# A shared expert cut into five parts per batch and handed out from a queue

## The chip, the cores and the metric

The kernel runs on one core of a Trainium2 chip. The metric is the device time of one execution in microseconds (us). The kernel before takes 3459.9 us, the median of three runs (3458.05 to 3460.16).

## The reference

Two decoder layers over a batch of 8 sequences of 256 tokens, width 512, all in 32-bit floats. Every layer adds attention, cross-attention and a feed-forward block to the running `x`, each behind a layernorm. The change lies in the feed-forward block of layer 0, a mixture of 64 experts with six chosen per token and a capacity of 192 tokens per expert, plus a shared expert that every token passes through:

```python
logits = x @ gate_weight.T          # softmax, best 3 of 8 groups, best 6 experts
slot = flat * C + jnp.minimum(pos, C - 1)
buf = jnp.zeros((E * C, H)).at[slot].set(x[tok]).reshape(E, C, H)
out = einsum(silu(buf @ Wg) * (buf @ Wu), Wd)
y = jnp.sum(out[slot] * topk_w, axis=1)
shared = jax.nn.silu(x @ Sg.T) * (x @ Su.T) @ Sd.T      # 512 -> 704 -> 512
return y + shared
```

Here `x` is the layernormed input of the block. `Sg` and `Su` are 704 x 512, `Sd` is 512 x 704.

## The kernel before

The kernel runs six stages one after the other: self-attention, cross-attention of layer 0 (`l0_cross`, which also carries the front half of the mixture), the experts (`l0_experts`), the state-space attention of layer 1 (`l1_mamba`), cross-attention of layer 1, and the last feed-forward block. `x` stays on the chip as 16 tiles of 128 tokens, two per batch.

Work is recorded in program order. A framework then orders the instructions of each engine; instructions given to `self.pin` (all matrix products, the products `hT`, the additions of the shared result to `x`, the shared weights' loads) keep the order in which the program records them. Each engine, and the DMA queue of SyncE (SP), runs its instructions in order.

`l0_cross` works in rounds, one per batch `b`, of eight slots `s`; there are 8 + 3 rounds, since later steps of a batch lag behind (L628 and on). A slot computes one part of the attention scores (`scores`: products, an exp on ScalarE, three VectorE passes), the outputs of the slot two before, and then what the list `between[s]` holds. An entry there is a pair: how far ahead or behind the round's batch it works, and the step. So `(1, turn)` transposes the next batch, `(-1, result)` projects the attention output of the batch before and adds it to `x` by way of ScalarE, VectorE and GpSimd, and `(-2, ...)` are the steps of the mixture's front (`l0_front`, L676) for the batch whose attention is done: `normal` (layernorm, and a copy to device memory), `turn` (transpose to `xnT`), `route` (gate products, top-k), `slots` (a place in the expert's buffer for every choice). `scatter` writes the tokens' numbers to two maps in device memory with indirect DMAs on GpSimd, two per call and twelve per batch; `last` adds one more behind the last batch and loads the maps, from which `slots` in the narrower sense, the list of tokens per expert, is summed.

The shared expert of a batch has six steps `hidden(b, m)` (L830), one per block of 118 of the 704 hidden features (the last has 114), and two steps `down(b, i)` (L846), one per 128 tokens. A hidden step is eight products into one bank, a silu on ScalarE and a product on VectorE; a down step is six products and an addition to `x`. The list `between` places them by hand: `hidden` 0 to 3 in slots 6 and 7 of round b + 2, 4 and 5 in slot 0 of round b + 3, the two downs in slots 2 and 3. Its weights are loaded once, ahead of the rounds, into four tiles of the weight pool (L683 to L696): Sg and Su in halves of 704 KB, and Sd in six slabs of 118 rows (the last 114) of 512 features; the first four slabs share the four tiles.

`l0_experts` takes the experts in pairs: it gathers the tokens (GpSimd, indirect), transposes them, loads each expert's weights through the same pool of eight tiles, and writes the results to `y_d` in device memory (L962, L977). `l1_mamba` then runs `combine` (L663) batch by batch: twelve indirect gathers of `y_d` per batch into a ring of six tiles `ye`, each added to `x` on VectorE. The layernorm of the first batch, with a power on GpSimd's queue (L153), and the transposes (L1040) follow.

Of the kernel before, what the change touches and what calls it, by code (L numbers as in the profile page):

```python
# [18 lines left out]
P = 128  # L19
# [49 lines left out]
class Decoder:  # L69
# [352 lines left out]
    def l0_cross(self, front):  # L422
# [11 lines left out]
        with ExitStack() as ctx:  # L434
# [169 lines left out]
            for i in range(2):  # L604
# [4 lines left out]
            hidden = lambda m: [(-2 - m // 4, lambda b, m=m + i: moe["hidden"](b, m)) for i in range(2)]  # L609
            between = (  # L610
                [(1, lambda b: features(b, "k", 0)), *hidden(4)],
                [(1, lambda b: features(b, "k", 1)), (1, lambda b: values(b, 0))],
                [(-3, lambda b: moe["down"](b, 0)), (1, lambda b: values(b, 1)), (-2, moe["normal"])],
                [(-3, lambda b: moe["down"](b, 1)), (1, turn)],
                [(-1, lambda b: divide(b, 0)), (1, lambda b: features(b, "q", 0)), (-2, moe["turn"])],
                [(-1, lambda b: divide(b, 1)), (-2, moe["route"]), (1, lambda b: features(b, "q", 1)), (2, context)],
                [(-1, lambda b: result(b, 0)), *hidden(0), (-2, moe["slots"])],
                [(-1, lambda b: result(b, 1)), *hidden(2)],
            )

            for n in range(6):
                s, i, k = (7 + n) % 8, n // 3, n % 3 * 2
                between[s].append((
                    -2 if s == 7 else -3,
                    lambda b, i=i, k=k: moe["scatter"](b, i, k) if b < B - 1 else None,
                ))

            for b in range(B + 3):  # L628
                for s in range(8):
# [7 lines left out]
                    for d, work in between[s]:  # L637
                        if 0 <= b + d < B:
                            work(b + d)
                            if work is moe["slots"] and b + d == B - 1:  # L640
                                for n in range(6):
                                    moe["scatter"](B - 1, n // 3, n % 3 * 2)
                                moe["last"]()

# [3 lines left out]
    def l0_moe(self, outer):  # L648
# [9 lines left out]
        self.l0_cross(lambda *pools: self.l0_front(*pools, xn_d, topw, read, slots))  # L658
        with ExitStack() as ctx:
            self.ps = ctx.enter_context(self.psum("ps"))  # L660
            self.l0_experts(ctx.enter_context(self.pool("c2")), xn_d, slots, y_d)
# [14 lines left out]
    def l0_front(self, one, pool, bank, xn_d, topw, read, slots):  # L676
# [3 lines left out]


        n_m = -(-MS // MB)
        rows = lambda m: min(MB, MS - m * MB)  # L683
        up, sd = {"g": [], "u": []}, []
        for n, name in (("g", "Sg"), ("u", "Su")):
            for c in range(2):
                t = self.wpool.tile([P, 2048], F32, tag="w", name="w")
                v = t[:, : 2 * MS].rearrange("p (c m) -> p c m", c=2)
                self.pin(nc.sync.dma_start(v, a[name][2 * c * P : 2 * (c + 1) * P, :].rearrange("(c p) m -> p c m", p=P)))
                up[n].append(v)  # L690
                m = len(sd)
                sd.append(t[:MB, 2 * MS : 2 * MS + D])
                self.pin(nc.sync.dma_start(sd[m], a["Sd"][m * MB : (m + 1) * MB, :]))
        for m in range(4, n_m):
            sd.append(one.tile([P, D], F32, name=f"sd{m}")[: rows(m), :])
            self.pin(nc.sync.dma_start(sd[m], a["Sd"][m * MB : m * MB + rows(m), :]))  # L696
# [3 lines left out]
        zero = one.tile([P, NSC], I32, name="zero")  # L700
# [20 lines left out]
        def turn(b):  # L721
            xnT = work[b]["xnT"] = pool.tile([P, HC, S], F32, tag="mT", name="mT", bufs=1)
            for i, xn in enumerate(work[b]["xn"]):
# [4 lines left out]
                nc.scalar.copy(xnT[:, :, i * P : (i + 1) * P], t.rearrange("p (c t) -> p c t", c=HC))  # L728

# [11 lines left out]
        def slot(b):  # L741
# [3 lines left out]
            pos = pool.tile([P, 2, E0], F32, tag="pos_e", name="pos_e", bufs=1)  # L745
# [12 lines left out]
            past = pool.tile([P, 2, E0], F32, tag="past", name="past", bufs=1)  # L758
# [70 lines left out]

        def hidden(b, m):  # L830
            w = work[b]
            if m == 0:
                w["hT"] = pool.tile([P, n_m, S], F32, tag="hT", name="hT", bufs=1)
            n = rows(m)
            t = bank()
            for h, name in enumerate("gu"):
                for c in range(HC):
                    self.mm(
                        t[:n, h * S : (h + 1) * S], up[name][c // 2][:, c % 2, m * MB : m * MB + n],
                        w["xnT"][:, c, :], c == 0, c == HC - 1,  # L840
                    )
            act = pool.tile([P, S], F32, tag="act", name="act")
            nc.scalar.activation(act[:n], t[:n, :S], AF.Silu)
            self.pin(nc.vector.tensor_tensor(w["hT"][:n, m, :], act[:n], t[:n, S:], ALU.mult))  # L844
# [795 lines left out]
```

## Time and profile before

| What | us |
|---|---|
| median of three runs | 3459.9 |
| the profiled execution | 3465.64 |
| its span | 3463.9 |
| cross-attention of layer 0 with the mixture's front, 415.6 to 1149.3 | 733.7 |
| TensorE busy in it | 669.2 |
| experts, 1149.3 to 1951.7 | 802.4 |
| TensorE busy in it | 802.4 |
| behind the experts to mamba's first transposes, 1951.7 to 1980.3 | 28.6 |

The profile is of one execution. TensorE is busy for 3247 of 3463.9 us, VectorE for 1598.5, ScalarE for 998.6, GpSimd for 758.5. A row of the profile names an engine (PE is TensorE, DVE VectorE, ACT ScalarE, POOL GpSimd, SPq the DMA queue of SyncE), the line of the kernel, the operation and the tiles it writes and reads. All matrix products stand under L100, the helper that records them, and count twice in "x"; tell them apart by their tiles: `mm<-mT,w` are the shared expert's hidden products, `mm<-w,hT` and `mm<-sd,hT` its downs, `sc<-xgT,w` the experts'. What stands in square brackets is the engine's idle time just before the row, and what ended it.

### The profile page before, as it was taken

To read this page: it belongs to the slowest core of one execution; us is meant where nothing else is said; L and a number is where in the kernel's file an instruction comes from. 1 tells how busy PE (TensorE), PEld (TensorE's weight loads), DVE (VectorE), ACT (ScalarE), POOL (GpSimd) and SP (SyncE) were. 2 spreads that over 40 slices of the span, in tenths; PEclk is the share of its full clock that TensorE was granted. 3 is DMA by queue.
4 is the path that set the end of the run, shared out by engine and by line. 5 is a ranking of instruction groups with operands and counts; after the bars stand their busy time and mean duration, and the time that the engine had idled before them with its cause. 6 is when DMAs were issued, how large, how long until landed. Compare 5 with 4: busy or idle time off the path is not lost.

```text
span 3463.9 us, 47107 instructions
## 1 busy us (share of the span) xinstructions
PE 3247.0 (94%) x18803; PEld 2114.8 (61%) x18803; DVE 1598.5 (46%) x3784; ACT 998.6 (29%) x1959; POOL 758.5 (22%) x792
## 2 busy tenths in 40 slices
PE   7999878999999899999999578998999899999999
PEld 5666545666666687878787455563444566666665
DVE  4555589888875000000000288655666333333332
ACT  1222223333342122222222133442555322222221
POOL 3222001222235211111110276322121111111111
PEclk9999989999999999999999778997999899999999
DMA  4000010000100677777777743011000000000000
GB/s 175 1 1 1 7 64 16 13 13 13 35 7 21 198 234 236 237 236 242 232 245 224 223 140 91 1 33 50 26 26 17 34 7 6 7 7 1 7 6 13
DMA packets 106812, 272.57 MB, mean 79 GB/s; under 512 B 15136, under 2 KB 23968, under 8 KB 105696
## 3 DMA queue, kind: packets, MB, share of 16 engines
q1 hardware_dynamic: 88128, 219.16, 19.3%
q0 software_dynamic: 18464, 50.40, 5.2%
q8 instruction: 148, 2.42, 0.3%
q14 instruction: 72, 0.59, 0.1%
HBM read 235.81 MB, written 33.70 MB: 78 GB/s over the span
## 4 chain that ended last, share of the span: by engine, by line
PE 67%; DVE 12%; POOL 3%; issue 2%; DMA 2%; ACT 1%; SPq 0%; POOLq 0%; DVEq 0%; ACTq 0%
PE mm L100 18%; PE sc L100 15%; PE out L100 7%; PE w L100 6%; PE s L100 4%; PE a L100 3%; PE b L100 3%; PE sums L100 2%; PE acc L100 2%; PE st L100 2%; DVE e L526 1%; PE pt L926 1%; PE rt L100 1%; POOL ye L667 1%; DVE acc L1066 1%
## 5 line engine op out<-in xcount | busy, mean ns | idle before, releaser
L100 PE MATMUL sc<-xgT,w 128*112 128x192 f32 (+1 forms) x3072 | 529.6, 328 | 0.0
L100 PEld LDWEIGHTS sc<-xgT,w 128*112 128x112 f32 (+1 forms) x3072 | 497.4, 182 | 41.1 <-issue 40.9
L952 DVE TENSOR_TENSOR aT<-act,sc 112x192 f32<-112x192 f32 (+1 forms) x192 | 68.0, 354 | 741.3 <-ACT act L951 741.3
L100 PE MATMUL mm<-xnT,w 128*128 128x256 f32 x1152 | 280.9, 401 | 7.4 <-ACT xnT L252 5.9
L100 PE MATMUL mm<-w,aT 112*128 112x512 f32 (+3 forms) x768 | 262.7, 596 | 0.0
L100 PEld LDWEIGHTS mm<-xnT,w 128*128 128x128 f32 x1152 | 227.2, 201 | 46.2 <-ACT xnT L252 8.2
L100 PE MATMUL w<-xnT,w 128*128 128x256 f32 x1024 | 242.9, 380 | 0.0
L100 PE MATMUL out<-w,mix 128*128 128x512 f32 x512 | 240.4, 592 | 0.0
L1483 DVE TENSOR_TENSOR h<-base,b 128x512 f32<-128x512 f32 x128 | 88.0, 687 | 327.4 <-PE b L100 327.4
L916 POOL DMA_INDIRECT xg<-xn_d,slots x96 | 90.9, 947 | 641.2 <-PE pt L926 634.8
L100 PEld LDWEIGHTS w<-xnT,w 128*128 128x128 f32 x1024 | 192.2, 190 | 61.1 <-issue 40.7
L1487 POOL TENSOR_TENSOR mix<-h 128x256 f32<-128x256 f32 x128 | 93.1, 727 | 610.4 <-DVE h L1485 549.6
L1344 DVE TENSOR_REDUCE m<-s 128x1 f32<-128x512 f32 x256 | 164.6, 685 | 102.3 <-PE s L100 83.5
L153 POOL TENSOR_TENSOR lnr<-lne,c_nhalf 128x1 f32<-128x1 f32 x112 | 66.6, 596 | 645.7 <-DVE lne L151 639.5
L100 PE MATMUL st<-q,k 32*128 32x256 f32 (+1 forms) x1024 | 196.6, 545 | 1.2 <-ACT e L522 1.2
L100 PE MATMUL mm<-mT,w 128*118 128x256 f32 (+1 forms) x768 | 175.2, 388 | 9.8 <-DVE hT L844 9.8
L1293 ACT ACTIVATE e<-st 128x512 f32<-128x512 f32 x256 | 138.9, 595 | 141.9 <-PE st L100 140.2
L951 ACT ACTIVATE act<-sc 112x192 f32<-112x192 f32 (+1 forms) x192 | 63.6, 331 | 402.0 <-PE sc L100 402.0
L100 PEld LDWEIGHTS out<-w,mix 128*128 128x128 f32 x512 | 97.3, 190 | 122.4 <-issue 120.5
L100 PEld LDWEIGHTS mm<-w,aT 112*128 112x128 f32 (+3 forms) x768 | 95.6, 163 | 122.5 <-issue 122.5
L100 PEld LDWEIGHTS mm<-mT,w 128*118 128x118 f32 (+1 forms) x768 | 141.9, 186 | 45.9 <-DVE hT L844 12.1
L100 PE MATMUL s<-k,q 32*128 32x512 f32 x512 | 159.9, 700 | 6.3 <-issue 3.5
(333 smaller groups left out, 5315.1 us busy)
## 6 DMA issues: line engine op xcount, KB each, us to landing
w<-in_Wg SPq DMA_DIRECT2D x64, 704.0 KB, 7.7
w<-in_Wu SPq DMA_DIRECT2D x64, 704.0 KB, 4.6
w<-in_Wd SPq DMA_DIRECT2D x64, 448.0 KB, 6.4
w<-in_Wd SPq DMA_DIRECT2D x64, 256.0 KB, 5.4
y_d<-yo SPq DMA_DIRECT2D x64, 256.0 KB, 3.9
y_d<-yo SPq DMA_DIRECT2D x64, 128.0 KB, 4.1
w<-in_W SPq DMA_DIRECT2D x8, 1024.0 KB, 5.5
x<-in_x SPq DMA_DIRECT2D x16, 256.0 KB, 5.8
```

What stands on the lines that cost most here:

```text
L100: self.pin(self.nc.tensor.matmul(out, lhs, rhs, start=start, stop=stop))
L153: ins = nc.gpsimd.tensor_tensor(r, e, self.nhalf[:, :n], ALU.pow)
L526: self.pin(nc.vector.scalar_tensor_tensor(e, e, 1.0, low, ALU.max, ALU.mult))
L667: nc.gpsimd.indirect_dma_start(y, None, y_d, bass.IndirectOffsetOnAxis(ap=read[:, k, i : i + 1], axis=0))
L916: nc.gpsimd.indirect_dma_start(xg, None, xn_d, bass.IndirectOffsetOnAxis(ap=slots[:, i : i + 1], axis=0))
L926: self.pin(nc.tensor.transpose(t[:, blk], w[n][:, blk], self.ident))
L951: nc.scalar.activation(act[:n_m], ps[:n_m, :CAP], AF.Silu)
L952: nc.vector.tensor_tensor(w["a", h][:n_m, m, :], act[:n_m], ps[:n_m, S : S + CAP], ALU.mult)
L1293: nc.scalar.activation(w["e"][kc][:, j, :], st, AF.Exp, scale=SCALE)
L1344: nc.vector.tensor_reduce(m, sc, AX.X, ALU.max)
L1483: nc.vector.tensor_tensor(both(h), twice(base), both(t), ALU.add)
L1487: nc.gpsimd.tensor_tensor(mix, h[:, :G], h[:, G:], ALU.add)
```

## The change

The eight steps become five parts: three of two hidden steps each and two downs (`shared_parts`). The parts of batches 0 to 6 wait in one queue, in order. The list `between` has four places `(0, None)`, in slots 0, 2, 6 and 7; from slot 7 of round 2 on each takes the next part from the queue. When the last batch's `slots` and `scatter` are recorded (round 9, slot 6), what is left in the queue is recorded behind them. The last batch's parts are not in the queue: its `xnT` is written to device memory, read back in the experts' stage, the shared weights are loaded once more behind the last expert's, and its five parts stand behind the last expert.

To make room, several small tiles share the buffer of others: `zero`, `pos_e`, `past`, the silu's output (from two buffers to one, `gated`), and the transposes of the last two batches (in the ring of the softmax tiles). The transposes of the other batches get two buffers.

The diff, cut to its core (deleted functions moved unchanged are left out):

```diff
-            hidden = lambda m: [(-2 - m // 4, lambda b, m=m + i: moe["hidden"](b, m)) for i in range(2)]
             between = (
-                [(1, lambda b: features(b, "k", 0)), *hidden(4)],
+                [(1, lambda b: features(b, "k", 0)), (0, None)],
                 [(1, lambda b: features(b, "k", 1)), (1, lambda b: values(b, 0))],
-                [(-3, lambda b: moe["down"](b, 0)), (1, lambda b: values(b, 1)), (-2, moe["normal"])],
-                [(-3, lambda b: moe["down"](b, 1)), (1, turn)],
+                [(0, None), (1, lambda b: values(b, 1)), (-2, moe["normal"])],
+                [(1, turn)],
...
-                [(-1, lambda b: result(b, 0)), *hidden(0), (-2, moe["slots"])],
-                [(-1, lambda b: result(b, 1)), *hidden(2)],
+                [(-1, lambda b: result(b, 0)), (0, None), (-2, moe["slots"])],
+                [(-1, lambda b: result(b, 1)), (0, None)],
             )
...
+            parts = iter([
+                lambda b=b, work=work: work(b) for b in range(B - 1) for work in self.shared_parts(*moe["shared"])
+            ])
...
                     for d, work in between[s]:
-                        if 0 <= b + d < B:
+                        if work is None:
+                            if 8 * b + s >= 23:
+                                next(parts, lambda: None)()
+                        elif 0 <= b + d < B:
                             work(b + d)
                             if work is moe["slots"] and b + d == B - 1:
                                 for n in range(6):
                                     moe["scatter"](B - 1, n // 3, n % 3 * 2)
                                 moe["last"]()
+                                for part in parts:
+                                    part()
...
         def turn(b):
-            xnT = work[b]["xnT"] = pool.tile([P, HC, S], F32, tag="mT", name="mT", bufs=1)
+            xnT = work[b]["xnT"] = pool.tile([P, HC, S], F32, tag="mT" if b < B - 2 else "e", name="mT", bufs=2 if b < B - 2 else 3)
...
+            if b == B - 1:
+                nc.sync.dma_start(end, xnT)
...
-            act = pool.tile([P, S], F32, tag="act", name="act")
+            act = pool.tile([P, S], F32, tag="gated", name="gated", bufs=1)
             nc.scalar.activation(act[:n], t[:n, :S], AF.Silu)
-            self.pin(nc.vector.tensor_tensor(w["hT"][:n, m, :], act[:n], t[:n, S:], ALU.mult))
+            self.pin(nc.vector.tensor_tensor(made["hT"][:n, m, :], act[:n], t[:n, S:], ALU.mult))
+
+        def two(b, m):
+            hidden(b, m)
+            hidden(b, m + 1)
...
+        return (
+            *(lambda b, m=m: two(b, m) for m in range(0, n_m, 2)), *(lambda b, i=i: down(b, i) for i in range(2)),
+        )
...
                 late = [lambda pair=pair, h=h: first(pair, h)]
                 if h == 1:
                     late.append(lambda pair=pair: last(pair))
+        weights = self.shared_weights(pool)
+        xnT = pool.tile([P, HC, S], F32, tag="xnT", name="xnT", bufs=1)
+        nc.sync.dma_start(xnT, end)
         for work in late:
             work()
+        for part in self.shared_parts(pool, lambda: self.bank("sc"), weights, lambda b: xnT):
+            part(B - 1)
```

`shared_weights` issues the ten loads that `l0_front` issued before, in the same order: half of Sg, a slab of Sd, the other half, a slab, the same with Su, then the last two slabs, all pinned.

## The prediction

> **What bounds the kernel now.** I read the page, then the engines' busy time in stretches, then each engine's instructions in order around the two places where the change puts work.
>
> ```profile
> PE 3247.0 (94%) x18803; PEld 2114.8 (61%) x18803; DVE 1598.5 (46%) x3784; ACT 998.6 (29%) x1959; POOL 758.5 (22%) x792
> ...
> PE 67%; DVE 12%; POOL 3%; issue 2%; DMA 2%; ACT 1%; SPq 0%; POOLq 0%; DVEq 0%; ACTq 0%
> ```
>
> TensorE carries two thirds of the chain that ended last, so work removed from it can pay, but only where VectorE isn't as full. The cross-attention round of batch 4 (719.95 to 805.5, 85.5 us), cut at its eight slots; the columns are stretch, length, then busy time (count) of PE, weight load, DVE, ACT and POOL, granted clock, DMA share, GB/s:
>
> ```profile
> 740.88:751.31 10.43, 10.43 (x46) 4.44 (x45) 9.27 (x18) 1.03 (x1) 3.41 (x4) 1.00 0.01 1
> 751.31:759.18 7.87, 7.87 (x46) 3.86 (x45) 5.53 (x13) 1.98 (x4) 1.12 (x2) 1.00 0.10 35
> 774.80:788.90 14.10, 13.42 (x77) 9.09 (x78) 13.11 (x37) 3.80 (x6) 0.00 (x0) 1.00 0.06 20
> 788.90:805.50 16.60, 14.12 (x68) 9.03 (x67) 14.24 (x31) 9.31 (x16) 4.48 (x4) 0.90 0.00 0
> ```
>
> These are slots 2, 3, 6 and 7. Over the round PE is busy 82.1, DVE 71.0; slots 3 to 7 take 54.2 and hold 47.0 of DVE. TensorE bounds the round, with DVE close behind in its second half. The two gaps in TensorE's order of work around the experts:
>
> ```profile
> 1112.86 13.98 PE L100 MATMUL mm<-mT,w 128*118 128x256 f32 x64
> 1149.29 2.88 PE L926 MATMUL pt<-c_const,xg 128*128 128x128 f32 x12 [12.14 <-DMA xg<-xn_d,slots]
> ...
> 1946.25 5.47 PE L100 MATMUL mm<-w,aT 128*128 128x512 f32 x18
> 1980.32 1.11 PE L1040 MATMUL pt<-c_const,xn 128*128 128x128 f32 x4 [28.60 <-DVE xn L169]
> ```
>
> 12.1 us are idle before the experts and 28.6 behind them. In the second, the combine runs on POOL and DVE (its first add, its seventh gather):
>
> ```profile
> 1964.63 0.75 DVE L670 SCALAR_TENSOR_TENSOR x<-ye,topw,x 128x512 f32<-128x512 f32 x1 [17.46 <-DMA ye<-y_d,read]
> ...
> 1969.45 1.17 POOL L667 DMA_INDIRECT ye<-y_d,read  x1 [0.30 <-issue]
> ```
>
> And the shared weights, loaded once in the cross stage (SP's order; the stretch while only the tail of these loads is under way; landing):
>
> ```profile
> 445.30 0.41 SPq L689 DMA_DIRECT2D w<-in_Sg  x1
> 454.40 5.52 SPq L689 DMA_DIRECT2D w<-in_Su  x1
> ...
> 468.00:472.00 4.00, 4.00 (x39) 2.06 (x41) 3.90 (x7) 2.17 (x5) 0.00 (x0) 1.00 0.13 50
> w<-in_Sg SPq DMA_DIRECT2D x2, 704.0 KB, 11.0
> w<-in_Su SPq DMA_DIRECT2D x2, 704.0 KB, 16.6
> ```
>
> DMA share 0.13 at 50 GB/s is two of 16 engines. The last Su lands 454.4 + 16.6 = 471.0, 25.7 us behind the first issue; the stream is dry at about 482. SP held the first Su back to 452.7 for its buffer, but these two engines never ran empty (51 GB/s at 456 to 460, with nothing else in flight), so the hold doesn't set the landing.
>
> **The price of one batch's shared expert.** Batch 7's lies bare at 1103.94 to 1137.1: six hidden blocks 7.0 + 13.9 = 20.9, two down products 10.5 (1126.68 on), 31.4 us of PE. A pair of blocks is 7.0, a down 5.2.
>
> **Front: up to the last attention result.** Ahead of result(7,1) (ends 1076.3) TensorE now does six batches and a pair, 6 x 31.4 + 7.0 = 195.4. After, 24 parts stand there: four batches, three pairs and a down, 125.6 + 26.2 = 151.8. So 43.6 us leave TensorE. Not all is gained. Per round 5.2 leave slot 3, and a pair in 6 or 7 becomes a down (1.8) or slot 2's down a pair (-1.8). Slots 3 to 7 then hold 42 to 46 us of PE beside 46.3 of DVE (hT and x adds move with the parts, 0.41 and 0.69 each). Round 2 (546 to 634), which has little shared work, shows that regime: its slots 3 to 7 took 63.1 for 56.7 of DVE, 90%. 46.3/0.9 = 51.4, so a round gains 2.8 there, at best 5.2. By round: 2 (round 2, slot 6 is DVE's: 16.46 of 17.80), 3, 3, 4.5, then 6.4 in round 6 (no context to clean, DVE 66 of 80), 4.3 in round 7 (slot 3 falls back on the exp-DVE chain, as slots 1 and 2 now do), 4.7 in round 8: 27.9. The gate tile has one buffer, not two: the second silu waits for the first product and the next exp stands behind it on ACT, 1 to 1.5 us where DVE lags; I take 3 for all. 25 gained; bounds 15 (DVE at 90% everywhere) and 43.6 (TensorE bounds all).
>
> **Front: from there to the experts.** result(7,1) to the slots products is 34.6 us now (1076.3 to 1110.9) and stays: it is the layernorm chain of x (POOL's pow at +21.6 behind the scatters), then top-k; TensorE has 19.4 us to do under it (a down, two pairs), so it idles some 4 us, +1 for a half clock. Behind the slots stand seven parts in the built program, five of batch 6 and two downs of batch 5: 1.9 + 31.4 + 10.5 = 43.8. Now the experts start 38.3 behind the slots (1111.0 to 1149.3), waiting for 13 scatters, the map and the gather. So +5.5; but without the idle gap the first expert isn't at half clock: x48 took 9.62 against 8.05, x12 2.88 against 1.8, -2.6. Net +3.9. **Experts start 25 - 3.9 = 21 us earlier.** Nothing of the shared expert is issued on POOL; ACT, with 239 of 734 us busy in this stage, takes its silus between exps as before. Hidden: the write of xnT (512 KB, on SP ahead of the map's loads, done before the scatters), its read (512 KB at 236 GB/s, 2 us, where the DMA share is 0.74), the tags reused by zero, pos_e and past (freed a round before); uncovered they would cost 2 us each.
>
> **Back.** Times as if the experts had not moved. The ten shared loads (4.3 MB) are pinned behind the y_d write of 1941.86, so they issue from 1942.2, and the last two y_d writes, Wz, Wxbc and wout stand behind them on SP's queue. When does the second Su land? Row one, the expert weights on this queue: 4.6 to 7.7 us from issue to landing, 360 to 386 GB/s in the stretch 1936 to 1944; so the 3.6 MB up to that Su by 1955, and TensorE runs straight on and ends at 1983.8. Row two, the same loads at 445: +25.7, so 1967.9. The Trainium skill decides ("DMA: Bandwidth & Descriptors", in "Why a DMA increments its semaphore by 16 and not by 1"): a copy uses the largest number of engines up to 16 that divides its slowest dimension. Sd comes in slabs of 118 rows, 2 x 59, so two engines: 242 KB at 49 GB/s is 4.9 us each, and Sg and Su have a sixteenth on these engines, behind them. That is a property of the load, not of the cross stage. I take row two. It also lets the y_d writes land only near 1979 (36.7 behind, as the stream at 482), not at 1961.
>
> Beside that batch 7 brings six silus on ACT (2.1 of 28.6 us busy there) and 3.8 us on DVE. Wz to wout now issue one by one as the Sd slabs land, the last near 1976, and take some 5.6 us each; mamba first needs them behind 2012: hidden, and worth that wait if mamba were to start before 1985.
>
> TensorE: gate of block 0, then idle to 1967.9; 0.9 + 17.5 for the rest of the blocks, 10.5 down. Clock: rows show half clock lasting on after a gap, 8.85 for 7.07 (711.2), 5.89 for 3.70 (986.9), 616.5 to 622.7: 1.8 to 3.1 lost. The skill ("TensorE: Matmul & The Clock Gate", Part 1) gives one window of 3.4 us, 1.7 lost. I take the rows, 2.4. End 1999.2. On DVE's queue both x adds stand ahead of all the combine's adds (built order): the first is at 2000.2, not 1964.63. Six gathers fit the buffers; the seventh waits for the first add: 2000.95 against 1969.45, +31.5. The pow behind the thirteenth gather, xn and mamba's first transposes follow at the same pace: **mamba starts at 2011.8, +31.5.** W1 (4 MB) now loads at 1996 to 2010 beside the gathers; gathers beside weights took 6.5 us against 3.7: +2 (0 to 4). Behind that everything keeps its order. **Back +33.5** (28 to 40).
>
> **Sum.** -21 + 33.5 = +12.5 on the profiled 3465.6 (span 3463.9 and 1.7 around it): 3478.1. The median of the runs is 5.7 lower: 3459.9 + 12.5 = **3472.4**.
>
> **Rivals.** (A) The shared weights land as expert weights do, by 1955: first add at 1984.7, seventh gather 1985.5, +16 and 2.5 of contention; -21 + 18.5 = -2.5, 3457.4. Against it: the rows at 445. (B) Not slower: TensorE bounds the whole front, as PE 82.1 of 85.5 in round 4 suggests; 43.6 - 3.9 = 39.7, less 33.5: -6.2, 3453.7. It decides once the front gains over 37.4. Against: DVE at 13.1 of 14.1 and 14.2 of 16.6. With (A) too it would be -21. (C) DVE sets the front's pace fully and the half-clock gaps multiply: gain 15 - 3.9 = 11; +22.5, 3482. (D) The parts don't fill the gaps at all: the seven only lengthen the wait, batch 7's only follows its weights; that is the forecast's own reading behind the experts, and with a front of 15 it is (C).
>
> **How the numbers follow.** Forecast 0.57, C 0.18, A 0.13, B 0.12 (half of it with A's arrival in part). 0.2% is 7 us, about what a measurement can tell. Faster: a third of A and half of B, 0.10; same: the rest of A and B and the forecast's low edge, 0.19; slower 0.71. Range from A, 3457, to past C with a back of 37: 3486. The likeliest's own: 3464 to 3481.
>
> **What would show it.** Right: experts start near 1128, PE has no gap ahead of them; behind them PE waits some 14 us for DMA w<-in_Su within the first hidden block; x_83's add stands ahead of the first combine add, 35 us later after the experts' end than now; PE idle ahead of mamba falls to about 12. Wrong: Su landing within 14 us of the first issue; rounds 3 to 5 shorter by over 6 or under 2 us; any wait of the experts on weights (e1's now load without the 12 us lead).

## The result

| | before | after |
|---|---|---|
| median of 6 runs, us | 3461.28 (3458.05 to 3465.86) | 3487.75 (3483.22 to 3490.96) |
| profiled execution, its span | 3465.64, 3463.9 | 3487.53, 3485.8 |

After / before is 1.0076 (95% interval 1.0065 to 1.0087): **26.5 us slower**. The forecast was +12.5. Executions of one kernel differ by some 4 us to either side, so a difference of a few us between two medians of four runs shows nothing here.

The profiled execution of before reached the cross stage 4.6 us later than that of after (first score product at 441.68 and 437.08), in a stage that the change doesn't touch. Stages are therefore compared by their lengths. Five points of the trace cut the time: the first score product of the cross stage, the end of result(7,1), the end of the first 48 expert products, the end of the last expert product, mamba's first transposes.

| stretch | before | after | difference | forecast |
|---|---|---|---|---|
| cross stage up to result(7,1) | 634.8 | 622.0 | -12.8 | -25 |
| result(7,1) to the end of the first expert products | 85.1 | 92.2 | +7.1 | +3.9 |
| experts | 790.1 | 790.1 | 0 | 0 |
| last expert product to mamba's transposes | 28.6 | 60.4 | +31.8 | +31.5 |
| from there to the end | 1483.5 | 1483.9 | +0.4 | +2 |
| sum | | | +26.5 | +12.5 |

The sum equals the difference of the medians. So the back, the last two stretches, came near its forecast (+32.2 for +33.5), and the front, the first two, gained 6 us where 21 were expected.

The page of after, engines and chain:

```profile
PE 3254.9 (93%) x18803; PEld 2117.2 (61%) x18803; DVE 1595.2 (46%) x3784; ACT 990.0 (28%) x1953; POOL 764.4 (22%) x792
...
PE 64%; DVE 14%; issue 3%; POOL 2%; DMA 2%; ACT 2%; SPq 0%; POOLq 0%; DVEq 0%; ACTq 0%
```

TensorE has the same 18803 products as before, but is busy 7.9 us longer, and its share of the chain fell from 67% to 64%: waits on DVE and half clock took the place of products.

**The front.** Round 4 of after, slots 2 to 7, each cut 0.7 us behind the slot's first score product (columns: stretch, length, then busy time and count of PE, weight load, DVE, ACT and POOL, granted clock, DMA share, GB/s):

```profile
724.57:737.17 12.60, 12.44 (x70) 7.90 (x72) 11.97 (x24) 2.69 (x3) 2.45 (x3) 1.00 0.01 2
737.17:742.14 4.97, 3.02 (x38) 1.56 (x40) 4.32 (x9) 3.44 (x6) 0.97 (x1) 1.00 0.01 0
742.14:754.81 12.67, 7.72 (x55) 5.81 (x52) 10.84 (x22) 3.59 (x7) 6.33 (x6) 0.82 0.12 44
754.81:764.13 9.32, 9.32 (x72) 6.47 (x68) 6.47 (x24) 2.69 (x8) 2.21 (x2) 0.88 0.09 28
764.13:777.95 13.82, 13.51 (x81) 9.12 (x82) 12.92 (x34) 3.10 (x5) 0.00 (x0) 1.00 0.06 20
777.95:791.96 14.01, 10.96 (x51) 4.28 (x52) 13.34 (x28) 7.50 (x12) 5.11 (x4) 1.00 0.00 0
```

Slots 4 and 5 of the same round before:

```profile
759.18:766.74 7.56, 7.25 (x53) 5.36 (x52) 7.16 (x13) 3.01 (x6) 4.38 (x4) 1.00 0.10 35
766.74:774.80 8.06, 8.06 (x65) 6.35 (x65) 6.98 (x22) 2.73 (x8) 2.33 (x2) 1.00 0.11 33
```

Slot 2 grew from 10.43 to 12.60 (a pair where a down stood), slot 3 fell from 7.87 to 4.97, and slot 4 grew from 7.56 to 12.67, of which TensorE works 7.72. The clock drops there and stays down in slot 5. The round took 89.1 us against 85.5, with one part less. What TensorE waited for in rounds 3 to 5 of after (engine and instruction, releaser, us in total, times, longest), and below the dots the counterpart of the first line before:

```profile
PE mm L722 <- DVE o L569: 14.4, 3, 5.0
PE mm L100 <- DVE hT L875: 5.5, 3, 2.5
PE st L100 <- ACT e L522: 2.4, 2, 1.2
PE mm L100 <- ACT raw L496: 2.4, 1, 2.4
...
PE mm L727 <- DVE o L569: 0.9, 3, 0.3
```

The first line is where most of the added waiting lies: the second transposes of the layernormed x in slot 4 wait for DVE's o product, 4.4 to 5.0 us in each round (0.9 in all three before). Over the three rounds TensorE's idle time went from 10.4 to 28.7 us. And ACT's waits in the same rounds:

```profile
ACT gated L874 <- DVE hT L875: 25.6, 5, 7.7
```

Five times the second silu of a pair waits up to 7.7 us for the first product, with the next exp behind it. Before the change the silus wait only for TensorE (`ACT act L843 <- PE mm L100`).

**Up to the experts and behind them.** TensorE's order in after:

```profile
1064.08 13.98 PE L100 MATMUL mm<-mT,w 128*118 128x256 f32 x64
1082.50 1.09 PE L722 MATMUL mm<-c_const,xn 128*128 128x128 f32 x4 [4.45 <-DVE xn L169]
...
1141.43 1.09 PE L960 MATMUL pt<-c_const,xg 128*128 128x128 f32 x8 [0.78 <-DVE x L886]
...
1951.31 2.06 PE L100 MATMUL sc<-xnT,w 128*118 128x256 f32 x4 [5.37 <-DMA w<-in_Su]
1958.03 20.32 PE L100 MATMUL sc<-xnT,w 128*118 128x256 f32 x84 [4.65 <-DMA w<-in_Su]
...
2001.86 1.11 PE L1079 MATMUL pt<-c_const,xn 128*128 128x128 f32 x4 [13.20 <-DVE xn L169]
```

The gap of 12.1 us ahead of the experts is gone. Behind them TensorE waits 10.0 us for the two halves of Su (and 1.9 for Sg, not shown), and 13.2 us ahead of mamba. The first combine add and the seventh gather stood 12.9 and 17.7 us behind the last expert product before; now it is 47.8 and 48.9:

```profile
1988.69 0.69 DVE L886 TENSOR_TENSOR x<-x,sc 128x512 f32<-128x512 f32 x1 [4.47 <-PE sc L100]
1989.29 4.68 DVE L681 SCALAR_TENSOR_TENSOR x<-ye,topw,x 128x512 f32<-128x512 f32 x6
...
1990.31 1.34 POOL L678 DMA_INDIRECT ye<-y_d,read  x1 [10.00 <-DVE x L681]
```

SP's queue at the shared loads of after (its second column is how long an issue held the queue), and a stretch of the stream:

```profile
1932.01 0.39 SPq L837 DMA_DIRECT2D w<-in_Sg  x1
1942.04 4.65 SPq L837 DMA_DIRECT2D w<-in_Su  x1
1948.31 10.44 SPq L837 DMA_DIRECT2D sd<-in_Sd  x2
1960.75 1.24 SPq L1011 DMA_DIRECT2D y_d<-yo  x2
...
1952.00:1956.00 4.00, 1.37 (x4) 0.53 (x2) 0.00 (x0) 0.00 (x0) 0.00 (x0) 0.50 0.13 49
```

TensorE resumes on the last Su at 1958.03, 26.0 us behind the first issue; the stretch 1952 to 1956 moved 49 GB/s at a DMA share of 0.13, which is two engines of 16. The last y_d writes are issued only at 1960.75.

### The profile page after: what moved, and what is told of

It reads as the page before. It is cut to its first block, busy times and chain, and to the rows that moved or that the text cites. A ratio compares the mean times of both kernels' runs of the same rounds, so it can differ in the third digit from the quotient of the medians.

```text
span 3485.8 us, 47130 instructions
## 1 busy us (share of the span) xinstructions
PE 3254.9 (93%) x18803; PEld 2117.2 (61%) x18803; DVE 1595.2 (46%) x3784; ACT 990.0 (28%) x1953; POOL 764.4 (22%) x792
## 3 DMA queue, kind: packets, MB, share of 16 engines
q1 hardware_dynamic: 90224, 224.53, 19.7%
## 4 chain that ended last, share of the span: by engine, by line
PE 64%; DVE 14%; issue 3%; POOL 2%; DMA 2%; ACT 2%; SPq 0%; POOLq 0%; DVEq 0%; ACTq 0%
PE mm L100 16%; PE sc L100 15%; PE out L100 7%; PE w L100 6%; PE s L100 4%; PE a L100 3%; PE b L100 3%; PE sums L100 2%; PE acc L100 2%; PE st L100 2%; DVE e L526 2%; PE pt L960 1%; PE rt L100 1%; DVE acc L1105 1%; DMA ye<-y_d,read 1%
## 5 line engine op out<-in xcount | busy, mean ns | idle before, releaser
L100 PE MATMUL sc<-xgT,w 128*112 128x192 f32 (+1 forms) x3072 | 528.0, 327 | 0.0
L100 PEld LDWEIGHTS sc<-xgT,w 128*112 128x112 f32 (+1 forms) x3072 | 495.8, 181 | 41.0 <-issue 40.9
L100 PE MATMUL mm<-xnT,w 128*128 128x256 f32 x1152 | 279.6, 399 | 7.4 <-ACT xnT L252 5.9
L100 PE MATMUL mm<-w,aT 112*128 112x512 f32 (+3 forms) x768 | 262.7, 596 | 0.0
L100 PEld LDWEIGHTS mm<-xnT,w 128*128 128x128 f32 x1152 | 226.3, 200 | 46.0 <-ACT xnT L252 8.3
L100 PE MATMUL w<-xnT,w 128*128 128x256 f32 x1024 | 242.9, 380 | 0.0
L100 PE MATMUL out<-w,mix 128*128 128x512 f32 x512 | 240.4, 592 | 0.0
L100 PEld LDWEIGHTS w<-xnT,w 128*128 128x128 f32 x1024 | 192.2, 190 | 61.1 <-issue 40.7
L100 PE MATMUL st<-q,k 32*128 32x256 f32 (+1 forms) x1024 | 198.2, 552 | 8.0 <-ACT e L522 7.7
L100 PEld LDWEIGHTS out<-w,mix 128*128 128x128 f32 x512 | 97.3, 190 | 122.4 <-issue 119.8
L100 PEld LDWEIGHTS mm<-w,aT 112*128 112x128 f32 (+3 forms) x768 | 95.6, 163 | 122.5 <-issue 122.5
L100 PE MATMUL s<-k,q 32*128 32x512 f32 x512 | 159.9, 700 | 6.3 <-issue 3.5
L100 PE MATMUL mm<-mT,w 128*118 128x256 f32 (+1 forms) x672 | 152.8, 386 | 7.5 <-DVE hT L875 4.1
L100 PEld LDWEIGHTS mm<-mT,w 128*118 128x118 f32 (+1 forms) x672 | 122.8, 184 | 39.4 <-issue 5.7
```

Of the source, the lines that this page charges most:

```text
L100: self.pin(self.nc.tensor.matmul(out, lhs, rhs, start=start, stop=stop))
```

## The experiments

Two questions: why four parts per round at new places cost more than five at the old ones, and what the 32 us behind the experts consist of. For the front the table gives the length from the first score product to the end of the first expert products (719.9 before, 714.2 after), for the back the length from the last expert product to the first score product of the second cross stage, less the 446.5 of before (+31.9 after). These lengths are of the one profiled execution of each kernel, the medians of all its executions. The runs that leave work out, the repeat of after and the first run of d_defer stand in the text.

| run | median, us | over before (95%) | front | back |
|---|---|---|---|---|
| a_five | 3492.18 | 1.0096 (1.0079 to 1.0112) | 714.9 | +31.1 |
| a_inplace | 3479.75 | 1.0059 (1.0042 to 1.0076) | 704.1 | +31.6 |
| a_pair5 | 3494.86 | 1.0094 (1.0077 to 1.0111) | 720.8 | +30.7 |
| a_mb128 | 3480.33 | 1.0059 (1.0042 to 1.0076) | 716.4 | +16.0 |
| d_defer2 | 3486.16 | 1.0069 (1.0053 to 1.0084) | 712.3 | +28.6 |
| c_all | 3468.86 | 1.0027 (1.0017 to 1.0037) | 714.3 | +9.6 |
| c_five | 3469.62 | 1.0029 (1.0019 to 1.0039) | 715.6 | +10.0 |
| e_best | 3461.56 | 0.9999 (0.9991 to 1.0008) | 705.7 | +11.3 |
| e_best2 | 3455.40 | 0.9992 (0.9983 to 1.0001) | 705.6 | +4.7 |

### The old places, five per round

```
-                [(1, turn)],
+                [(0, None), (1, turn)],
...
-                            if 8 * b + s >= 23:
+                            if 8 * b + s >= 22:
```

> The kernel after with five parts per round (one more in slot 3) from slot 6 of round 2: each pair and each down of batches 0 to 6 then stands where it stood before the change, and only batch 7's shared expert stays behind the experts. Nothing is left out. If the account of the two profiles holds (the new places of the parts gain 5.7 us up to the experts, the work behind them costs 32): time before + 32 = about 3493, rounds 3 to 5 at 85.5 each, experts start no later than before, and behind the last expert product the same 60 us to mamba's first transposes as in the kernel after. Rival (the shared tags and the gate tile cost by themselves, not the places): rounds 3 to 5 at 87 to 89 as in the kernel after, and 3500 or more.

Measured 3492.18, which is 31.9 above before. Rounds 3 to 5 took 85.52, 85.53 and 85.46, so the shared tags and the gate tile cost nothing in these rounds at the old places. The back is nearly the same as in after. Taking batch 7 out of the tail gained 5.0 us up to the experts by itself, because they then wait only for their gather: TensorE stood 29.4 us idle for it. What the queue adds to that in after is 0.7 us in the traces and 4 to 5 us in the medians: it is 11.6 us shorter up to result(7,1) and 10.9 longer from there, where seven parts now stand. **As built, with its one-buffer gate tile, the redistribution is worth little, though it took 43.6 us of TensorE from the stretch up to result(7,1).**

### No parts at all

```
-                            if 8 * b + s >= 23:
-                                next(parts, lambda: None)()
+                            pass
...
-                                for part in parts:
-                                    part()
```

> The kernel after without the shared expert of batches 0 to 6: no part is taken from the queue, neither in the rounds nor behind the last slots (left out: that share of the result; batch 7's stays behind the experts). It measures what the parts cost in the rounds. The forecast's picture (a round is PE's sum, with DVE at 90% as floor): rounds 3 to 5 at DVE 66.5/0.9 = 74, 11.5 below the 85.5 that they take with 31.4 us of parts, so that a fifth of the parts is worth at least 2.3 per round. Other picture (DVE and the chains through ACT pace slots 2 to 5 even with no part in them): rounds at 78 to 82, slots 2 to 4 at 20 or more with PE idle there, so that a part hidden well costs under 1.5 and a fifth of them is worth nothing that a badly placed pair doesn't take back. Experts then start on their gather alone, 27 to 29 us behind the slots' products, where the kernel after had parts.

Rounds 3 to 5 took 70.5, 71.7 and 71.6 (one execution, like that of the four parts below). One of them (columns as above):

```profile
681.68:753.37 71.69, 55.60 (x340) 33.34 (x339) 64.79 (x148) 21.90 (x42) 27.65 (x24) 0.83 0.05 16
```

DVE is busy 64.8 of 71.7, 90%: the forecast's ratio holds for a round without parts, and the other picture (78 to 82) is refuted. The clock is down to 0.83 in it, so some of TensorE's 55.6 are slower products. Five parts at the old places therefore cost 14 us of time for 31.4 of TensorE, 2.8 each on average. The experts started on their gather, with TensorE 29.9 us idle. Up to the end of the first expert products this kernel took 640.9 us: the 35 parts of after, 220 us of TensorE, cost 73.

### Four parts, none of them moved

```
-                                next(parts, lambda: None)()
+                                part = next(parts, lambda: None)
+                                if s != 3:
+                                    part()
```

(on top of the five-per-round edit; it leaves out each batch's second down product)

> The kernel with five parts per round at their places before the change, but the part of slot 3 (each batch's second down product with its x add) is left out for batches 0 to 6: four parts per round, 26.2 us of TensorE instead of 31.4, and none moved (left out: the shared expert's share of each second half batch but the last). With five parts these rounds take 85.5, with none 70.5 to 71.7, with four at the places of the kernel after 88.0, 89.1 and 86.7. Theory P (the new places cost, not the number of parts): rounds 3 to 5 at 80.3 to 82.7, as the forecast had it for a part that leaves and moves nothing. Theory C (slot 3 without its down loses the cover of the layernorm chain, and PE waits there instead): 84 to 86, PE waits 4 us or more in slot 4.

Rounds 3 to 5 took 84.63, 86.07 and 84.62, against 85.5 with five parts: leaving out a down product of 5.2 us gained 0.9, -0.5 and 0.8. Theory C's lengths hold, but not its place: slot 4 kept its length (7.74 for 7.57), and the time came back in slots 5 and 6. Round 4, slots 3 to 6:

```profile
746.59:749.26 2.67, 2.67 (x34) 1.59 (x33) 2.46 (x5) 1.89 (x4) 0.00 (x0) 1.00 0.00 0
749.26:757.00 7.74, 7.25 (x53) 5.36 (x52) 6.04 (x15) 3.08 (x6) 3.21 (x4) 1.00 0.19 69
757.00:769.99 12.99, 11.37 (x62) 8.85 (x61) 11.78 (x37) 2.66 (x7) 4.52 (x5) 0.74 0.08 21
769.99:784.70 14.71, 13.51 (x75) 9.18 (x74) 11.88 (x28) 3.42 (x5) 0.00 (x0) 1.00 0.06 19
```

and TensorE's order in slot 5:

```profile
760.34 1.13 PE L100 MATMUL mm<-r,norm 128*128 128x256 f32 x4 [1.62 <-DVE o L569]
761.31 2.73 PE L100 MATMUL mm<-c_small,mT 128*128 128x64 f32 x16
763.83 6.22 PE L100 MATMUL mm<-xnT,w 128*128 128x256 f32 x16
```

TensorE comes 5 us early, waits 1.6 for DVE's o, and then runs slower: 2.73 and 6.22 us for products that take 1.89 and 3.67 at full clock (before, 769.36 and 771.09), with the granted clock down to 0.74 over the slot. Slot 5 is 5.0 us longer than before, nearly all that slot 3 gave. TensorE is busy 80.3 in this round; before less the down product makes 76.9.

### The gate tile

```
-            act = pool.tile([P, S], F32, tag="gated", name="gated", bufs=1)
-            nc.scalar.activation(act[:n], t[:n, :S], AF.Silu)
-            self.pin(nc.vector.tensor_tensor(made["hT"][:n, m, :], act[:n], t[:n, S:], ALU.mult))
+            act = made["hT"][:n, m, :]
+            nc.scalar.activation(act, t[:n, :S], AF.Silu)
+            self.pin(nc.vector.tensor_tensor(act, act, t[:n, S:], ALU.mult))
```

> The kernel after, but the silu of a hidden block is written into its place in hT and multiplied there, so that the one-buffer gate tile is gone. Nothing is left out. Theory G (the gate tile): in the profile after, ACT stands 5.7 to 7.7 us between the two silus of a pair put in slots 0 and 2, because the second waits for the first product at its turn on DVE, and the next exp stands behind it. Without that, the exps of the slots behind come some 2 us earlier; slots 2 to 4 of rounds 3 to 5, which took 29.0, 30.2 and 27.0 us, fall by about 2 each and slot 0 by up to 3: 8 to 12 us in all, about 3477. Theory D (DVE's own order bounds slots 2 to 4 and the waits of ACT lie beside it): 0 to 2 us, 3486 to 3488, and the 4.4 to 5.0 us for which PE waits at the layernorm's transposes stay. Either way nothing changes behind the experts: first combine add 48 us behind the last expert product.

3479.75, 8.0 below after (7.0 when each is set against before as measured beside it), and 10.2 less up to the end of the first expert products. Rounds 3 to 5 took 84.52, 87.49 and 84.08 for 87.30, 89.07 and 86.65. In ACT's order of slot 2 of round 4 the second silu now waits for TensorE alone, and the exp starts when its scores are there:

```profile
727.69 0.38 ACT L874 ACTIVATE hT<-mm 118x256 f32<-118x256 f32 x1 [2.29 <-PE mm L100]
731.15 0.38 ACT L874 ACTIVATE hT<-mm 118x256 f32<-118x256 f32 x1 [3.07 <-PE mm L100]
731.55 1.28 ACT L522 ACT_TABLE_LOAD   x1
735.25 1.02 ACT L522 ACTIVATE e<-st 128x1024 f32<-128x1024 f32 x1 [2.42 <-PE st L100]
```

Theory G holds by its sum, and in two rounds by its place: slots 2 to 4 take 2.0 us less in round 3, 3.1 in round 4 and nothing in round 5. What theory D said of the transposes holds too: their waits stay, 13.5 us in three rounds for 14.4. Of the 10 us, 6.9 came in rounds 3 to 5 and 3.3 between the start of round 7 and the last result. The three rounds are still only 0.5 us shorter in sum than with five parts.

With this edit the queue's front is 10.9 us shorter than that of the run with five parts per round (704.1 for 714.9), and the median 12.4 lower. So much of what the redistribution could gain went into the gate tile. Whether five per round would gain by the same edit was not run; that its rounds 3 to 5 take 85.5 with one gate buffer, as before with two, speaks against it.

### The pair out of slot 2

```
+                            if s == 2:
+                                wait = bool(parts) and parts[0][0] < 3
-                            if 8 * b + s >= 23:
+                            if 8 * b + s >= 23 and parts and not (s == 2 and wait) and not (s == 5 and not wait):
```

(slot 5 gets an entry in the table; parts carry their number)

> The kernel after, but in slot 2 the queue gives only a down product; where a pair of hidden blocks is next, it goes to the end of slot 5 of the same round. Same number of parts per round, nothing left out. Theory P (a pair in slot 2 delays exp on ACT and the products on DVE, and with them the wait of PE in slot 4): slots 2 to 4 of rounds 3 to 5, which took 29.0, 30.2 and 27.0 us, fall to about 20, as in round 6, where slot 2 had a down and took 20.9 with it; slot 5 grows by 7; per round -1 to -3, and the half clock behind the wait is gone: 3 to 8 us in all, 3480 to 3485. Theory C (slot 3 lost the cover: DVE paces slots 2 to 4 whatever PE does there): slots 2 to 4 stay at 25 or more, PE waits 7 us longer in slot 4, slot 5 grows by 7: 3 x 5 us slower, about 3500.

3494.86, 7 slower than after by the medians, though its four executions spread over 12 us (3488.88 to 3500.82) and the intervals of the two overlap. Rounds 3 to 5 did shorten, to 86.79, 84.79 and 84.96, and slots 2 to 4 to 22.6, 22.5 and 19.7; the last is what theory P said, the others lie between the two. From round 7 to the last result it lost 4.1 us against after, and behind that result 7.7 more: there the same edit took the second of the two pairs that lie in the layernorm's wait (13.98 us at 1064.08 in after) to a place behind it. TensorE waited 11.9 us for the last xn, for 4.45, and ran the pairs behind the wait in 16.5 us for 14.0. The place mends the rounds in part and uncovers the tail; a run without the second effect was not made.

### The slabs

```
-MS, MB = 704, 118
+MS, MB = 704, 128
```

> The kernel after with blocks of 128 rows of the shared expert's inner dimension (five of 128 and one of 64) in place of 118 (five of 118 and one of 114). As many blocks, loads and products. Nothing is left out. Theory E (slabs of 118 rows go on two of 16 DMA engines and hold the stream at 49 GB/s): now every slab goes on 16, no stretch near 50 GB/s is left in these loads, the last Su lands some 14 to 17 us behind the first issue instead of 26, PE waits under 4 us for it instead of 10, and the y_d writes behind it land before 1960. Mamba's first transposes come 9 to 14 us earlier: 3474 to 3479. Rival (the stream is held by the buffers of w that the last experts free): landing hardly changes, 3483 to 3488. The cross stage is to stay the same under both.

3480.33, 7.4 below after, just outside the 3474 to 3479 expected. The profiled execution (3473.23) is 14.3 below that of after and has 15.9 us less behind the experts; the other three (3479.62 to 3481.78) gained about half of that, which no trace explains. In the trace TensorE doesn't wait for a shared weight any more. The stretches from the first issue (1933.75) on:

```profile
1933.75:1937.00 3.25, 3.25 (x22) 3.25 (x21) 0.35 (x1) 0.33 (x1) 0.00 (x0) 1.00 0.85 221
1937.00:1941.00 4.00, 4.00 (x16) 2.00 (x16) 0.35 (x1) 0.84 (x2) 0.00 (x0) 1.00 1.04 409
1941.00:1945.00 4.00, 4.00 (x21) 2.12 (x18) 0.00 (x0) 0.66 (x2) 0.00 (x0) 1.00 1.03 395
1945.00:1949.00 4.00, 4.00 (x20) 3.29 (x19) 0.42 (x1) 0.39 (x1) 0.00 (x0) 1.00 1.05 364
```

No stretch at 50 GB/s is left, TensorE works through, and the first gather is issued at 1950.09, 6.9 us behind the last expert product, for 31.7 in after. Theory E is shown for the landing and the waits; its size in the median is half of what this trace has. What stays, +16.0: TensorE works for 32.3 us behind the last expert product, the first combine add comes 33.0 behind it, and mamba waits for that chain.

### The order of the x adds

```
             for b in range(-4, B):
+                if b == -2:
+                    rest(lambda: bank("sc"))
                 for work, ahead, *more in round_:
```

(`rest` runs batch 7's two downs; hT lies in a buffer of w)

> The kernel after, with batch 7's two down products and their x adds taken behind the combine of batches 0 and 1 in the order of work (ahead of mamba's first transposes on PE); the hidden blocks stay where they are, hT lies in a buffer of w. Nothing is left out. Theory O (the order on DVE: both x adds ahead of every combine add): the first combine add then waits only for the last hT product, 37.4 us behind the last expert product instead of 47.9; mamba's first transposes come some 9 to 10 us earlier, 3477 to 3480. Rival (the y_d writes that land only 31 us behind the last expert product, and the gathers behind them, set the first combine add anyway): under 4 us, 3484 to 3488.

The first time, 3486.09 (1.0078, 1.0063 to 1.0094), while its trace had mamba's transposes 7.6 us nearer to the experts. So it was run again with the kernel after beside it.

> The kernel with batch 7's down products behind the combine of batches 0 and 1 once more. Its trace has mamba's first transposes 52.8 us behind the last expert product and the second 64.6 behind it, against 60.5 and 70.8 in the kernel after, but the median was only 1 to 2 us lower. If the trace is typical, it is 6 us below the kernel after on this chip; if the order of the x adds is worth nothing beside the late y_d writes, the two are within 2 us.

> The kernel after as it is, for comparison on one chip with the next run: 3485 to 3490, and behind the last expert product 60.5 us to mamba's first transposes, 70.8 to the second.

3486.16 and 3487.28: 1.1 apart. The first combine add did come 10 us earlier, 37.5 behind the last expert product. But the first gather is still issued only 31.2 us behind it: it needs the y_d writes, which stand behind the shared loads on SP's queue and are issued at 1962.17. The later gathers run beside the weights of the second layer. TensorE:

```profile
1993.11 0.66 PE L1093 MATMUL pt<-c_const,xn 128*128 128x128 f32 x4 [2.91 <-DVE xn L169]
2008.11 1.09 PE L1093 MATMUL pt<-c_const,xn 128*128 128x128 f32 x4 [14.34 <-DVE xn L169]
```

The first transposes gain 10.5 us, the second 5.8, the end 1 to 3. So the places are those of theory O (37.4 and some 10 us), and the time is that of the rival (under 4 us). That the late y_d writes are the reason is likely but not isolated. Once the slabs no longer hold the stream, the order is worth more: +9.6 and +10.0 behind the experts in the next two runs, for +16.0 with 128 rows alone.

### The edits together

> The kernel after with three edits together: blocks of 128 rows, the silu written into hT, and batch 7's down products behind the combine of batches 0 and 1. Nothing is left out. If the account holds: -8 for the gate tile, -7 to -15 for the slabs, -10 for the order of the x adds: 3455 to 3462, the first combine add some 23 us behind the last expert product (22.0 for the last hT product in the kernel with blocks of 128) and mamba's first transposes some 35 us behind it, against 28.6 before the change and 60.5 after. If the edits overlap (the same wait counted twice) it stays above 3465.

3468.86, above the 3455 to 3462 expected. The back is as worked out: first combine add 22.0 us behind the last expert product, transposes 36.7, +9.6 in all. The front isn't: 714.3, although the silu lies in hT. With blocks of 128 rows that edit gained 2.1 us of front (716.4 with 128 rows alone), not 10; why was not traced.

> Blocks of 128 rows and batch 7's down products behind the combine of batches 0 and 1, as in the run of the three edits, but the parts of batches 0 to 6 five per round at their places before the change, gate tile as after. Nothing is left out. It says what the queue's places are worth once the back is mended: rounds 3 to 5 at 85.5, experts start on their gather as in the kernel with five per round; 3460 to 3468, that is 4 to 10 us above the run with three edits. If the places bring nothing, the two are within 3 us.

3469.62, within 1 us of c_all: with 128 rows, the queue's places and the silu in hT together bring nothing over five parts per round.

The next run keeps 118 rows and loads each slab as 112 rows and the rest:

```
+        def slab(dst, src, n):
+            load(dst[:112, :], src[:112, :])
+            load(dst[112:n, :], src[112:n, :])
...
+            if n == 2:
+                combine(pool, 0)
             parts[n](B - 1)
```

> The kernel after with the silu written into hT, slabs of 118 rows loaded as 112 and 6 rows (so that the blocks stay as they are but the stream goes on all engines), the combine of batch 0 placed ahead of the third pair of hidden blocks of batch 7, and batch 7's two down products behind mamba's first round of preparation. Nothing is left out. By the account: -8 for the gate tile (not seen again in the run of three edits, where the blocks had 128 rows; it has to come back here), and behind the experts the first combine add some 15 us behind the last expert product and mamba's first transposes some 28 to 32 behind it, as before the change: 3449 to 3460, below the kernel before. If the gate tile's gain was an accident of alignment, 3458 to 3466.

3461.56, level with before and above the 3449 to 3460 expected. The gate tile's gain is back (705.7). Mamba's transposes came 33.1 us behind the last expert product, but the two downs, now behind mamba's preparation, lay bare there for 11.6 us. TensorE had stood idle 10.2 us ahead of the transposes. So the last run splits batch 0's combine around the third pair and puts the downs into that gap:

> As the run that placed batch 0's combine ahead of the third pair (silu written into hT, slabs of 112 and 6 rows), but only the combine of x0 stands ahead of the third pair, that of x1 behind it, and batch 7's two down products stand ahead of mamba's first transposes, not behind mamba's preparation. Nothing is left out. In that run PE stood 10.2 us idle ahead of the transposes, and the two downs (11.5 to 13 us) lay bare 30 us later; the time was that of the kernel before. If bare PE work was what was left of the cost behind the experts, the downs now fill the idle 10 us: transposes again some 33 to 36 us behind the last expert product, nothing bare behind them, 3447 to 3454, below both kernels. If the preparation of mamba was held up by DVE's combine adds all the same and the downs only lay inside that wait, nothing is gained: 3458 to 3464.

TensorE's order:

```profile
1938.85 18.39 PE L100 MATMUL sc<-xnT,w 128*118 128x256 f32 x84 [1.99 <-DMA w<-in_Su]
...
1965.66 1.88 PE L100 MATMUL sc<-sd,w 118*128 118x512 f32 x4
1967.38 0.60 PE L1102 MATMUL pt<-c_const,xn 128*128 128x128 f32 x4
1969.35 0.63 PE L1102 MATMUL pt<-c_const,xn 128*128 128x128 f32 x4 [1.36 <-DVE xn L169]
```

TensorE runs from the last expert into mamba with 3.4 us of waits; the back costs +4.7 for +31.9 in after. 3455.40 is 3.9 below before, with an interval (0.9983 to 1.0001) that doesn't exclude no change, and short of the 3447 to 3454 expected. It is not shown to beat the kernel before. It does show that the 32 us were no price of the work itself: the same work stands behind the experts.

## Why the prediction was wrong

The direction and the back were right; the front term was twice too large, and the range ended 1.8 us short.

- **The step that failed is "Front: up to the last attention result".** It took 43.6 us off TensorE, held each round to DVE at 90%, and got 25; measured are 12.8. Two of its terms are wrong: what a part is worth in a round (27.9 in sum), and the gate tile (3).
- **What a part is worth.** The forecast let a part taken out gain 2.8 to 5.2 us in a round, as long as DVE's sum allowed it. At the old places the one part that was left out, a down product of 5.2 us, is worth 0.4 us on average over three rounds. Neither engine fills these rounds (in round 4 of after, TensorE is busy 78.3 and DVE 76.4 of 89.1); they wait for each other in turn. In round 4 of the four-part run, what one slot gave came back two slots later as a wait and slower products.
- **By round**: forecast 3, 3, 4.5 and 6.4 for rounds 3 to 6, measured -1.8, -3.5, -1.2 and +4.5; for the stretch from round 7 to the last result forecast 9.0, measured -0.1. The other way, round 2 gained 14.1 for 2. The forecast had called its slot 6 DVE's, since DVE was busy 16.46 of 17.80; without its pair the slot took 6.34, so that share was no floor. Slot 0 of round 3, which got the pair, gave back 5.0 (12.20 to 17.19).
- **The gate tile** was priced at 3. Without it the stretch up to the last result is 10.0 us shorter, and the median 7 to 8. Those 7 us too few are more than half of the 12 missing there. That the rest is no larger is luck: with the silu in hT this stretch is 22.8 us shorter than before, near the 27.9 of the rounds, but round 2 gives 14.0 of it for 2, and rounds 3 to 5 give 0.5 for 10.5.
- **A moved pair was priced at 1.8 us of TensorE.** In slots 2 to 4 of rounds 3 to 5, where slot 2 holds a pair, after takes 29.0, 30.2 and 27.0 us; in round 6, where it holds a down, 20.9. A pair also brings two silus with their table loads between two exps, and two products in DVE's order ahead of the o that the transposes wait for. Taking it out of slot 2 shortened the rounds by 6.5 us in sum. That it explains the rounds alone is not shown.
- **Half clock** was counted at the experts and behind them, not in the rounds. TensorE's products of rounds 3 to 5 are 17.4 us fewer by the prices of a pair and a down, its busy time only 11.8: some 5.6 us (an estimate) went into slower products, with the granted clock at 0.95 for 0.98.
- **Up to the experts**: forecast +3.9, measured +7.1. The seven parts and the lost idle gap were right (the first 48 products took 8.06 for 9.62). The stretch to the slots' products was taken as +1 for half clock and is 3.7 longer: behind a 4.45 us wait TensorE ran a pair in 8.43 us for 7.07, and the small products ahead of it in 5.70 for 3.23.
- **The back was right step by step.** TensorE resumed on the last Su 26.0 behind the first issue (25.7 forecast, with the median landing of both halves; the later one alone makes 25.4). Its 84 products behind that wait took 20.32, 1.9 more than the 18.39 in e_best2, where the forecast had 2.4 and set 1.7 aside. The first combine add stood 47.8 behind the last expert product (48.5), the seventh gather 48.9 (49.2), mamba's transposes 60.4 (60.1), contention afterwards 0.4 for 2. The rule of the Trainium skill behind it ("DMA: Bandwidth & Descriptors", "Why a DMA increments its semaphore by 16 and not by 1": the engines of a copy are the largest number up to 16 that divides its slowest dimension) is borne out by the run that changes only the rows, to 128, and by e_best2, which among other edits splits them into 112 and a rest: while these loads run, 364 to 409 GB/s in the first (from 1937 on) and 292 to 339 in the second (1928 to 1940) in place of 49, and waits of 0 and 2 us for Su in place of 10.
- **The rivals.** A (weights as fast as an expert's) is refuted for after; with 128 rows no wait is left and the back costs +16.0 in the trace, near A's +18.5. B (TensorE bounds the front) is refuted by the run with four parts, where 5.2 us less of TensorE gained 0.4. C (gain 15, 3482) had the nearest number and named the half clock, but not the reason: DVE doesn't fill the rounds. One sign set for being wrong, rounds 3 to 5 shorter by under 2 us, is what came: they grew by 6.5 in sum.

## What to carry to other kernels

Where two engines are both busy for most of a stage, as TensorE at 96% and DVE at 83% of these rounds, the price of a piece of work is what the stage loses when that piece alone is left out at its place, not its busy time; a run without any of it gives the floor. Before work is spread anew, look at what each piece puts into the in-order queues of the other engines at its new place, and how many buffers it has there. For a load behind which others stand, look at the GB/s of its tail: here slabs of 118 rows held the queue for all that followed.

## What the runs showed of the hardware

A wait of 1.6 us on TensorE, in a round that was otherwise nearly full, was followed by slower products (2.73 us for 1.89 and 6.22 for 3.67); in that slot the granted clock was 0.74, and the loss of 3.4 us was twice the wait. And the slabs of Sd that moved at 49 GB/s with 118 rows left no slow stretch with 128 rows: the stream ran at 364 to 409 GB/s right through them.
